# Loads of the next image's first two pairs of chunks, moved ahead by four steps of the image

## The chip, the cores and the metric

The kernel runs on one core of one Trainium2 chip. The metric is the time of one execution on the device in microseconds (us). Before the change it was measured in seven runs; the profile is of one further execution.

The engines are PE (matrix products and transposes), PEld (its weight loads), DVE (elementwise on vectors), ACT (activations), POOL (indirect gathers, powers) and SP (nothing but DMA issues). ACT and POOL issue DMAs as well.

## The reference

The input x is (4, 32, 128, 128) in float32: four images. Layer 0 turns each image into 128 channels of 64 x 64 = 4096 positions, and lets every position attend to every other. Layer 1 is linear attention and a mixture of experts, each on normalised tokens and added to its input. Cut to what matters:

```python
def _L0_conv_ref(x, gamma):                 # per image: q is 128 x 4096
    xs = x.reshape(B, C, h, R, w, R).transpose(0, 1, 3, 5, 2, 4).reshape(B, C * R * R, h, w)
    q = xs.reshape(B, C * R * R, hw)
    energy = jnp.einsum('bci,bcj->bij', q, q)
    d = jnp.sqrt(jnp.diagonal(energy, axis1=1, axis2=2))
    energy = energy / (d[:, :, None] * d[:, None, :])
    attn = jax.nn.softmax(energy, axis=-1)
    out = gamma * jnp.einsum('bcj,bij->bci', q, attn) + xs
...
t = t + linear_attention(_ln_t(t))          # 8 heads, K^T V first, no softmax
t = t + experts(_ln_t(t))                   # softmax router, best 2 of 8, weighted sum
```

## The kernel before

**Layer 0.** The 4096 positions of an image are cut into 8 chunks of 512 (NCH), each of 4 blocks of 128 (NJ). Two neighbouring chunks, a pair kc = 0 to 3, are made ready by `prep(b, kc, st)`:

- its first step issues four DMA loads of 128 KB into the tile xx, on SP's queue (L278, inside `load_tokens`);
- it passes some idle units (L298), and then makes two groups of four transposes on PE (tiles ptq, L312), which DVE copies to qT (L301);
- DVE squares and sums (L323, L324), POOL takes the inverse root (L163), and DVE scales the chunks by it (qs, L337);
- two groups of four PE transposes (ptn, L345) follow, which ACT copies to qn (L343).

The tile xx of images 1 to 3 has one buffer. Both qT and qn must stand before the image's rows use them.

`attend(b, st)` runs over the rows i = 0 to 7 of chunks. As the energies are symmetric, only the chunks jc up to i are computed. A step makes two products of qn with qn (pe, L557), takes exp on ACT (pr, L560), and adds pr times qT to the row's sum (po, L439). The other triangle needs the transposed exps: DVE transposes pr in 32 x 32 blocks into the tile F_i_jc (L368), SP stores F to memory in one DMA of 1 MB (blocks<-F, L482), and three ticks later it loads it back in six DMAs with the blocks exchanged (F<-blocks, L494). A while later (LAG, 57 blocks of the clock) PE multiplies F with qT (pg, L374, and L395 for the diagonal), and DVE adds that to the sum o (L384). There are six buffers of F. F_7_1 is the tile of row 7 and chunk 1, blocks_7_2 the store of F_7_2.

**Layer 1** of image b begins at t = 84 and runs on beside the rows of image b+1, one step every ten blocks of the clock. What meets the change is its DMAs: xn<-xs (L1022, SP) brings sorted rows, ys<-xn and ys<-result (L1044, SP) stores the experts' products, POOL gathers them (L1123), acc<-t (L1099) fetches the residual on ACT's queue, DVE adds (L1092, "combine"), and SP stores the output in four DMAs (out_dram<-acc, L1105). In image 0, `setup_sorting` also fills the buffer xs with rows of x by DMAs on ACT's queue (L153), and `input_rows` loads the tile T (L278 too).

**Order.** The main loop at the end of the kernel issues everything, in the order in which it runs. Its clock counts blocks of the image's products; t is that clock in per cent of the image. Generators such as `prep` are listed in `timed` as (generator, begin, end, count): from t = begin on, it is stepped at a rate of count steps for (end - begin) per cent. A pair of `yield` in `prep` is therefore one unit of time, and `idle(n)` passes n such units. Each engine then works its list off in order, and waits there for what an instruction needs. The DMAs of SP and ACT take turns on eight semaphores, in the order of the program; one is issued only when the one eight places ahead of it has landed.

The two lines that place the next image's first pairs are L1341 and L1342, beside the idle units of L298.

Of the kernel before, what the change touches and what calls it, by code (L numbers as in the profile page):

```python
# [22 lines left out]
def kernel(  # L23
# [111 lines left out]
    def setup_sorting():  # L135
        def iota(dst, pattern, part=0):
            nc.gpsimd.iota(
                dst, pattern=pattern, base=0, channel_multiplier=part, allow_small_or_imprecise_dtypes=True
            )

        iota(rank_below, [[1, P]], part=-1)
        nc.vector.tensor_scalar(rank_below, rank_below, 0.0, None, ALU.is_gt)
        iota(upto, [[1, E], [-1, E]])
        nc.vector.tensor_scalar(upto, upto, 0.0, None, ALU.is_ge)
        iota(tiles_of[:, 0, :], [[P, HR]])
        iota(tile_no[:, :, 0], [[1, NT]])
        yield
        yield

        rows = x.rearrange("b c h w -> (b c h) w")  # L150
        step = NT * P // 8
        for g in range(16):
            inst = nc.scalar.dma_start(xs[g // 8][ts(g % 8, step), :], rows[ts(g, step), :])  # L153
            xs_made[g // 8].append(inst.ins)
            yield
            yield
# [5 lines left out]
    def pow_neg_half(dst, src):  # L162
        pinned(nc.gpsimd.tensor_tensor(dst, src, neg_half.to_broadcast(list(src.shape)), ALU.pow))  # L163
# [13 lines left out]
    def idle(n):  # L177
        for _ in range(2 * n):
            yield

    def keep_running(n, pool=None, tag=None):

        bank = psum_t("spare") if pool is None else pool.tile([P, CH], F32, tag=tag, name="spare")
        for _ in range(n):
            nc.tensor.transpose(bank[:, :P], ident, ident)
# [4 lines left out]
    def hold(name, evict, alloc=psum_t):  # L190


        while len(held) >= banks[0]:
            held[0]()
        bank = alloc(name)

        def done():
            if done in held:
                held.remove(done)
                evict(bank)  # L200

        held.append(done)
        return bank, done
# [69 lines left out]
    def load_tokens(dst, b, k0, nk, queues=(nc.sync, nc.sync)):  # L273
        src = tokens(x, b)
        for r1 in range(2):
            for s in range(2):
                p0 = s * 64 + r1 * 32
                queues[r1].dma_start(dst[p0 : p0 + 32], src[s, r1, :, k0 : k0 + nk, :])  # L278


    def prep(b, kc, st):

        if b == 0:
            if kc == 0:
                st["all"] = big1.tile([P, 4, 8, HW2, 2], F32, tag="T", name="xx_0")
            xx = st["all"][:, kc]
        else:
            xx = xin.tile([P, 8, HW2, 2], F32, tag="xx", name=f"xx_{b}_{kc}")
        first = b == 0 and kc == 0
        load_tokens(  # L290
            xx.rearrange("p k w r -> p k (w r)"), b, 8 * kc, 8, (nc.sync, nc.scalar if first else nc.sync)
        )
        qT = qpool.tile([P, 2, NJ, P], F32, tag="qT", name=f"qT_{b}_{kc}")
        st.setdefault("qT", {})[2 * kc] = qT[:, 0]
        st["qT"][2 * kc + 1] = qT[:, 1]
        yield
        yield
        yield from idle(2 if b else 1)  # L298

        def load_half(g, pt):  # L300
            nc.vector.tensor_copy(  # L301
                qT[:, :, 2 * g : 2 * g + 2, :].rearrange("p s j (r c) -> p (j r) s c", c=64),
                pt.rearrange("p (m s c) -> p m s c", s=2, c=64),
            )

        for g in range(2):
            yield
            pt, done = hold(f"ptq_{b}_{kc}_{g}", partial(load_half, g))
            for jj in range(2):
                for r2 in range(2):  # L310
                    k = 4 * g + 2 * jj
                    nc.tensor.transpose(  # L312
                        pt[:, ts(2 * jj + r2, P)], xx[:, k : k + 2, :, r2].rearrange("p k w -> p (k w)"), ident
                    )
            yield
            done()
        yield
        yield
        ss = stat.tile([P, 2 * NJ], F32, tag="ss", name=f"ss_{b}_{kc}")
        rn = stat.tile([P, 2 * NJ, 1], F32, tag="rn", name=f"rn_{b}_{kc}")  # L320
        for s in range(2):
            sq = work.tile([P, NJ, P], F32, tag="qs", name=f"sq_{b}_{kc}_{s}", bufs=2)
            nc.vector.tensor_tensor(sq, qT[:, s], qT[:, s], ALU.mult)  # L323
            nc.vector.tensor_reduce(ss[:, ts(s, NJ)], sq, AX.X, ALU.add)  # L324
            if first:
                pow_neg_half(rn[:, ts(s, NJ), 0], ss[:, ts(s, NJ)])
            elif s == 1:
                pow_neg_half(rn[:, :, 0], ss)
            yield
            yield  # L330
        yield from idle(1)
        if first:
            keep_running(22, ps_g, "pg")
        scaled = []
        for s in range(2):
            qs = work.tile([P, NJ, P], F32, tag="qs", name=f"qs_{b}_{kc}_{s}", bufs=2)
            nc.vector.tensor_tensor(qs, qT[:, s], rn[:, ts(s, NJ)].to_broadcast([P, NJ, P]), ALU.mult)  # L337
            scaled.append(qs)
        for s, qs in enumerate(scaled):
            yield  # L340
            qn = npool.tile([P, CH], F32, tag="qn", name=f"qn_{b}_{2 * kc + s}")
            st.setdefault("qn", {})[2 * kc + s] = qn
            pt, done = hold(f"ptn_{b}_{kc}_{s}", lambda p, qn=qn: nc.scalar.activation(qn, p, AF.Copy))  # L343
            for j in range(NJ):
                nc.tensor.transpose(pt[:, ts(j, P)], qs[:, j, :], ident)  # L345
            yield
            done()
        yield
        yield
# [233 lines left out]
    def finish():  # L583

        while queued or late:
            yield
            tick[0] += 1
            turn_tick()
            clock[0] += 3 * NJ
            step_share()  # L590
            yield


    def input_rows(b, st):
        st["T"] = T = big1.tile([P, KT, D], F32, tag="T", name=f"T_{b}")
        nk = 4 if b == 0 else 8
        for k in range(0, KT, nk):
            load_tokens(T[:, k : k + nk, :], b, k, nk)
            yield
            yield  # L600
            yield from idle(1)
# [729 lines left out]
    timed = [(first, 0, 1, 4)]  # L1331
    for b in range(B):

        if b == 0:
            for kc, begin, end in ((1, 0, 5), (2, 6, 20), (3, 25, 45)):
                timed.append((prep(0, kc, states[0]), begin, end, 12))
            timed.append((setup_weights(), 46, 58, 9))
            timed.append((setup_sorting(), 58, 98, 17))
        if b + 1 < B:
            nxt = states[b + 1]  # L1340
            timed.append((prep(b + 1, 0, nxt), 65, 82, 13))  # L1341
            timed.append((prep(b + 1, 1, nxt), 87, 99, 13))  # L1342
        begin, end, count = (52, 94, 17) if b == 0 else (36, 47, 9)
        timed.append((input_rows(b, states[b]), begin, end, count))
        done = [0] * len(timed)
        start = clock[0]
        closing = None
        for half, _ in enumerate(chain(attend(b, states[b]), finish() if b == B - 1 else ())):
            if half % 2 == 0:
                t = 100 * (clock[0] - start) / UNITS  # L1350
                moved = []
                if closing is None and t > 84:
                    closing = layer1(b, states[b])
                    steady.append([closing.first_parts() if b == B - 1 else closing.all_parts(), clock[0]])
                for n, (steps, begin, end, count) in enumerate(timed):
                    if t >= begin and done[n] * (end - begin) < (t - begin) * count:
                        moved.append(steps)
                        done[n] += 1
                for stream in steady:
                    if clock[0] >= stream[1]:  # L1360
                        stream[1] = clock[0] + PACE
                        moved.append(stream[0])
            for steps in moved:
                next(steps, None)
        for steps, *_ in timed:
            for _ in steps:
                pass
        timed = []
        if b + 1 < B:
            timed.append((prep(b + 1, 2, nxt), 2, 20, 13))  # L1370
            timed.append((prep(b + 1, 3, nxt), 30, 50, 13))
# [43 lines left out]
```

## Time and profile before

| | us |
|---|---|
| median of 7 runs | 1696.12 |
| lowest and highest of them | 1694.2 and 1701.56 |
| profiled execution | 1698.16 |
| its span, first to last instruction | 1696.4 |
| mean granted PE clock in the span | 0.994 |
| PE waiting at ptq (L312) for xx | 11.1 in 3 places |
| PE waiting at ptn (L345) for qs | 7.0 in 3 places |
| PE waiting at pg (L374) for F<-blocks | 1.2 in 1 place |

The profile gives the busy time of each engine in the span, groups of like instructions by line, and for an engine's idle time what ended it. A line such as "PE ptq L312 <- DMA xx<-in_x_dram" is PE idle ahead of the matmul at L312 that writes ptq, until a load of xx landed. In a timeline, "x4" is four like instructions shown as one, and the bracket at the end is the idle time before it. SPq and ACTq are the queues' issuing instructions; their time is that of the issue, not of the transfer. The granted clock is PE's share of full speed. Of the three waits at ptq and at ptn, one each (5.8 and 0.9 us) lies at the start of the program, where image 0 is loaded.

### The profile page before, as it was taken

The numbers are of one execution on the slowest core, as the hardware profiler recorded it, in microseconds if no ns is written. First come the engines' busy times: TensorE is split into PE (matmuls) and PEld (weight loads), VectorE is DVE, ScalarE is ACT, GpSimd is POOL, SyncE is SP. The second block draws the span as 40 slices with busy tenths as digits, with TensorE's granted clock in tenths as the row PEclk, the third lists the DMA queues.
The fourth block names the chain that finished last, engine by engine and source line by source line (L and its number), as shares of the span: only waits on it lengthen the run. The fifth ranks groups of instructions, "written<-read, shape, count | busy, mean of one in ns | idle before, by whom it ended". The sixth has DMA issues, their size and how long they took to land.

```text
span 1696.4 us, 21941 instructions
## 1 busy us (share of the span) xinstructions
PE 1646.7 (97%) x5458; PEld 878.5 (52%) x5458; DVE 934.8 (55%) x2443; ACT 927.8 (55%) x2893; POOL 511.1 (30%) x553
## 2 busy tenths in 40 slices
PE   8999999999999999989999999999999999999888
PEld 5444444455554555545564455544555455554643
DVE  4434334367485335477478334557748633455686
ACT  3555445565565555546565555545556555555376
POOL 1000000011027425451014641544102742445167
PEclk9999999999999999999999999999999999999999
DMA  4554756754458778875457777886435966885001
GB/s 132 172 171 164 202 174 211 246 198 162 139 168 281 227 234 247 248 216 175 147 177 230 237 233 241 246 262 198 164 137 168 285 223 221 249 249 145 7 10 41
DMA packets 227341, 323.94 MB, mean 191 GB/s; under 512 B 31760, under 2 KB 155792, under 8 KB 213136
## 3 DMA queue, kind: packets, MB, share of 16 engines
q1 hardware_dynamic: 206704, 283.57, 52.9%
q0 software_dynamic: 12288, 25.19, 5.1%
q10 hardware_dynamic: 8224, 13.77, 2.8%
q8 instruction: 46, 0.75, 0.2%
q14 instruction: 79, 0.65, 0.1%
HBM read 152.28 MB, written 173.15 MB: 192 GB/s over the span
## 4 chain that ended last, share of the span: by engine, by line
PE 81%; DVE 8%; DMA 4%; ACT 3%; issue 1%; POOL 1%; SPq 1%; ACTq 0%; DVEq 0%; POOLq 0%
PE po L439 23%; PE pe L557 22%; PE pg L374 19%; PE pys L1058 3%; PE py L1207 2%; PE pg L395 2%; DMA F<-blocks 2%; PE pys L1065 2%; PE pat L803 1%; PE pgram L677 1%; ACT xn L645 1%; DVE df L710 1%; DVE F L368 1%; PE ptq L312 1%; PE ptn L345 1%
## 5 line engine op out<-in xcount | busy, mean ns | idle before, releaser
L560 ACT ACTIVATE pr<-pe 128x512 f32<-128x512 f32 (+1 forms) x576 | 322.4, 560 | 541.0 <-PE pe L557 501.0
L439 PE MATMUL po<-pr,qT 128*128 128x512 f32 (+3 forms) x1152 | 550.9, 560 | 3.9 <-ACT o L444 3.7
L557 PE MATMUL pe<-qn,qn 128*128 128x512 f32 x896 | 461.6, 597 | 1.9 <-ACT pr L560 1.6
L374 PE MATMUL pg<-F,qT 128*128 128x512 f32 x864 | 441.7, 593 | 2.0 <-DMA F<-blocks 1.2
L368 DVE STREAM_TRANSPOSE F<-pr 128x512 f32<-128x512 f32 x440 | 306.1, 702 | 150.6 <-ACT pr L560 141.3
L439 PEld LDWEIGHTS po<-pr,qT 128*128 128x128 f32 x1152 | 216.5, 191 | 250.3 <-issue 220.5
L379 ACT ACTIVATE junk<-F 128x512 bf16<-128x512 f32 x432 | 268.0, 620 | 2.3 <-DMA F<-blocks 1.4
L374 PEld LDWEIGHTS pg<-F,qT 128*128 128x128 f32 x864 | 164.3, 191 | 194.6 <-issue 178.4
L1123 POOL DMA_INDIRECT yb<-ys,place x192 | 185.7, 967 | 241.2 <-ACT pr L560 66.7
L996 POOL DMA_INDIRECT xs<-xn,place x192 | 185.6, 967 | 157.4 <-ACT pr L560 93.8
L557 PEld LDWEIGHTS pe<-qn,qn 128*128 128x128 f32 x896 | 154.9, 192 | 109.0 <-issue 101.4
L384 DVE TENSOR_TENSOR o<-o,pg 128x512 f32<-128x512 f32 x110 | 75.5, 686 | 204.3 <-PE pg L374 204.1
L163 POOL TENSOR_TENSOR rn<-ss,neg_half 128x8 f32<-128x8 f32 (+1 forms) x17 | 26.9, 1585 | 332.6 <-DVE ss L324 332.5
L560 ACT ACTIVATION_READ_ACCUMULATOR pr<-pe 128x1 f32 x576 | 111.9, 194 | 0.0
L1032 ACT ACTIVATE xn<-pys 128x256 f32<-128x256 f32 x120 | 45.2, 377 | 108.6 <-PE pys L1065 108.4
L163 POOL TENSOR_TENSOR rsf<-dm_f,neg_half 128x8 f32<-128x8 f32 (+1 forms) x15 | 26.2, 1746 | 235.1 <-DVE sv_f L637 235.1
L1058 PEld LDWEIGHTS pys<-ew_sb,xn 128*128 128x128 f32 x468 | 69.7, 192 | 46.5 <-issue 43.5
L557 PE MATMUL pe<-qn 128*128 128x512 f32 (+3 forms) x256 | 90.8, 437 | 0.7 <-ACT qn L343 0.7
L163 POOL TENSOR_TENSOR rsa<-dm_a,neg_half 128x8 f32<-128x8 f32 x16 | 26.4, 1648 | 191.0 <-DVE sv_a L637 190.6
L379 ACT ACTIVATION_READ_ACCUMULATOR junk<-F 128x1 f32 x432 | 83.0, 192 | 0.0
L1041 DVE COPY xn<-pys 128x256 f32<-128x256 f32 x60 | 25.4, 424 | 88.0 <-ACT xn L1032 86.4
L1041 DVE COPY result<-pys 128x256 f32<-128x256 f32 (+1 forms) x60 | 24.6, 410 | 88.9 <-ACT xn L1032 79.8
(216 smaller groups left out, 1672.2 us busy)
## 6 DMA issues: line engine op xcount, KB each, us to landing
blocks<-F SPq DMA_DIRECT2D x108, 1024.0 KB
F<-blocks SPq DMA_DIRECT2D x216, 192.0 KB
F<-blocks SPq DMA_DIRECT2D x216, 128.0 KB
xn<-xs SPq DMA_DIRECT2D x114, 128.0 KB
F<-blocks SPq DMA_DIRECT2D x216, 64.0 KB
below<-F SPq DMA_DIRECT2D x31, 384.0 KB
out_dram<-acc SPq DMA_DIRECT2D x128, 64.0 KB
xx<-in_x_dram SPq DMA_DIRECT2D x62, 128.0 KB
```

What stands on the lines that cost most here:

```text
L163: pinned(nc.gpsimd.tensor_tensor(dst, src, neg_half.to_broadcast(list(src.shape)), ALU.pow))
L368: f()
L374: nc.tensor.matmul(pg.rearrange("p (a f) -> p a f", a=4), st["qT"][i][:, ib, :], G[:, :, ib], start=(ib == 0), stop=(ib == NJ - 1),)
L379: nc.scalar.activation(junk, G[:, :, ib], AF.Copy, accum_out=st["sums"][:, NJ * i + ib, jc : jc + 1])
L384: nc.vector.tensor_tensor(o, o, pg.rearrange("p (a j c) -> p a j c", a=4, c=S), ALU.add)
L439: nc.tensor.matmul(row["po"][:, lo:hi], qT[blk // NJ][:, blk % NJ, :], w, start=start, stop=(row["left"] == 0))
L557: nc.tensor.matmul(pe[:, c0:], qn[jc][:, ts(j, P)], qn[i][:, c0:], start=True, stop=True)
L560: nc.scalar.activation(pr[:, c0:], pe[:, c0:], AF.Exp, accum_out=sums[:, t, i : i + 1]).ins
L996: inst = nc.gpsimd.indirect_dma_start(xs[h], offset(place[:, i, k : k + 1]), xn[:, k, :], None)
L1041: nc.vector.tensor_copy(result[:, :n], p[:, 2 * P : 2 * P + n * D].rearrange("p (j c) -> p j c", c=D))
L1058: nc.tensor.matmul(p[:, 2 * P + j * D : 2 * P + j * D + D], bufs[4 + g % 2][:, j, :], weights[:, bass.ds(begins[2 * (g % 2) + j], D)], sta ...
L1123: inst = nc.gpsimd.indirect_dma_start(yb[k // 4][:, i, k % 4, :], None, ys, offset(place[:, i, k : k + 1]))
```

## The change

In images 1 to 3, the pairs kc = 0 and 1 idle for six units instead of two between the loads and the first transposes. Their generators begin earlier by about as much, with 17 steps in the time from the new begin: the loads of kc = 0 go out from t = 60 instead of 65, those of kc = 1 from 83 instead of 87 (t of the image before). The transposes stay at about the same t: for kc = 0 the step number n falls at 65 + 17n/13 before and at 60 + 22(n + 4)/17 after; for kc = 1 at 87 + 12n/13 and 83 + 16(n + 4)/17. In all, 24 loads of 128 KB move: two groups of four while image 0, 1 and 2 is computed. Pairs kc = 2 and 3 and image 0's own pairs are as before.

```diff
@@ -295,7 +295,7 @@
         st["qT"][2 * kc + 1] = qT[:, 1]
         yield
         yield
-        yield from idle(2 if b else 1)
+        yield from idle((6 if kc < 2 else 2) if b else 1)
 
         def load_half(g, pt):
             nc.vector.tensor_copy(
@@ -1338,8 +1338,8 @@
             timed.append((setup_sorting(), 58, 98, 17))
         if b + 1 < B:
             nxt = states[b + 1]
-            timed.append((prep(b + 1, 0, nxt), 65, 82, 13))
-            timed.append((prep(b + 1, 1, nxt), 87, 99, 13))
+            timed.append((prep(b + 1, 0, nxt), 60, 82, 17))
+            timed.append((prep(b + 1, 1, nxt), 83, 99, 17))
         begin, end, count = (52, 94, 17) if b == 0 else (36, 47, 9)
         timed.append((input_rows(b, states[b]), begin, end, count))
         done = [0] * len(timed)
```

## The prediction

> **What bounds the kernel now.** I began with the page's busy times and its chain that ended last.
>
> ```profile
> PE 1646.7 (97%) x5458; PEld 878.5 (52%) x5458; DVE 934.8 (55%) x2443; ACT 927.8 (55%) x2893; POOL 511.1 (30%) x553
> PE 81%; DVE 8%; DMA 4%; ACT 3%; issue 1%; POOL 1%; SPq 1%; ACTq 0%; DVEq 0%; POOLq 0%
> ```
>
> PE is busy for 97% of the span, so only PE's gaps and its clock can move the end. Next I read what PE waits for, and what SP waits for.
>
> ```profile
> PE ptq L312 <- DMA xx<-in_x_dram: 11.1, 3, 5.8
> PE ptn L345 <- DVE qs L337: 7.0, 3, 3.1
> ...
> SPq L278 <- DMA xs<-in_x_dram: 21.9, 4, 6.3
> ...
> SPq L494 <- DMA acc<-t: 18.8, 5, 4.5
> ```
>
> The columns are total us, times, longest. Both PE rows belong to `prep`. The last two rows show that SP's issues wait for transfers issued by ACT with which they share no data. The lists of both kernels say why: the DMAs of SP and ACT, counted together in program order, take turns on eight semaphores, and each first waits for the one eight places ahead.
>
> PE's timeline gives the places (start, duration, idle time before in brackets):
>
> ```profile
> 717.17 1.02 PE L374 MATMUL pg<-F,qT 128*128 128x512 f32 x2
> ...
> 723.42 0.88 PE L312 MATMUL ptq<-ident,xx 128*128 128x128 f32 x4 [2.65 <-DMA xx<-in_x_dram]
> ...
> 747.85 1.12 PE L345 MATMUL ptn<-ident,qs 128*128 128x128 f32 x4 [3.09 <-DVE qs L337]
> ...
> 1127.61 0.72 PE L312 MATMUL ptq<-ident,xx 128*128 128x128 f32 x4 [2.64 <-DMA xx<-in_x_dram]
> ...
> 1150.35 1.03 PE L345 MATMUL ptn<-ident,qs 128*128 128x128 f32 x4 [3.09 <-DVE qs L337]
> ```
>
> Call the gaps at 723.42 and 1127.61 A: the chunk pair kc=1 of the next image isn't there. Call those at 747.85 and 1150.35 B: the scaled chunks come late from DVE. The chain around the first A and B and SP's queue there:
>
> ```profile
> 711.37 3.43 DMA acc<-t
> 715.25 0.43 SPq L278
> ...
> 718.03 5.25 DMA xx<-in_x_dram
> 723.42 0.88 PE ptq L312 x4
> 724.30 1.71 PE pe L557 x2
> 726.00 1.53 PE po L439 x2
> 727.54 0.86 PE pg L374 x2
> ...
> 732.09 0.68 DVE qT L301
> ```
>
> ```profile
> 708.47 2.74 SPq L494 DMA_DIRECT2D F<-blocks  x6
> 714.86 0.34 SPq L482 DMA_DIRECT2D blocks<-F  x1
> 715.25 3.28 SPq L278 DMA_DIRECT2D xx<-in_x_dram  x4
> ...
> 720.62 4.54 SPq L494 DMA_DIRECT2D F<-blocks  x6
> ```
>
> The store blocks<-F at 714.86 stands eight places behind the fetch acc<-t (L1099), which ACT issues at 711.37 and which lands at 714.80. SP stands still for it, and the four xx loads behind come late. In the chain, pe and po take 1.71 and 1.53 after the gap instead of 0.86 a pair. The granted clock says why (third figure from the end):
>
> ```profile
> 723.00:728.00 5.00, 4.58 (x10) 2.42 (x11) 3.13 (x7) 1.30 (x4) 0.96 (x1) 0.66 1.01 288
> 1127.00:1131.00 4.00, 3.39 (x13) 2.00 (x14) 2.56 (x7) 1.30 (x4) 0.82 (x1) 1.00 1.09 272
> ```
>
> After both B it is 0.66 too. So three of the four gaps were followed by a lower clock, and the fourth was not. One drop costs 0.85 (pe) + 0.67 (po) + 0.16 (ptq, 0.88 against 0.72 at full clock) = 1.7 us.
>
> **The change, part by part.** No arithmetic is added. Six groups of four 128 KB loads (24 issues on SP, 0.4 to 0.5 us each in these rows where none waits) go ahead in SP's queue; the instructions behind them keep their t. ACT's and POOL's lists are unchanged in order. PE's differs by one group of ptn moved three places behind, DVE's by the copy and scaling steps of `prep`.
>
> *Removed: A.* The kc=1 loads of images 2 and 3 now stand right behind F_7_0's six loads (700.0 and some 1105.0), 21 us ahead of their transposes. The slowest xx load near here took 6.7 us (715.73 to 722.38), so A goes: 2.65 + 2.64, and one clock drop: 1.7. Sum: -7.0.
>
> *Added: a wait at pg.* Four more DMAs ahead shift every semaphore slot by four until the old place. They pass out stores, ys stores, blocks_7_1 and F_7_1's loads. The slot of acc<-t, which blocks_7_2 had, falls to the first of F_7_1's six loads (L494). These had gone out at 708.47 and landed by 714.14, 3.0 us ahead of the pg at 717.17. Now they wait for acc<-t. ACT still issues this at 711.37, behind its exp; such fetches took 2.9 to 3.5 us, so it lands at 714.3 to 714.9. The nearest groups of six loads took 5.0 (361.42 to 366.43) to 6.2 us (731.34 to 737.54) from first issue to last landing: 719.3 to 721.1. PE waits 2.1 to 3.9 us; I take 3.0. In image 2 the fetch goes out at 1115.57 and pg stands at 1121.37, again 2.1 to 3.9. Behind the waiting loads on SP are blocks_7_2, out stores and F_7_2's loads; those go out no later than before, since SP stood at 714.86 anyway, and F_7_2 has over 2.5 us to spare. So: 2 x 3.0, and by the count of three gaps in four, 2 x 0.75 x 1.7 = 2.6. Sum: +8.6, bounds 4.2 and 11.2.
>
> *Moved on DVE: B.* Ahead of B, DVE works without a gap from 731.48 to 747.85. The list of the change has the copy qT L301 (732.09, 0.68 us) ahead of work that ran at 726, where DVE then idles 3.9 us until 731.48. So the backlog, and B, shrink by 0.65 each: -1.3. The rest, 2.4 us, is shorter than any gap seen to lower the clock or not; I halve its chance, 2 x 0.5 x 1.7 = -1.7. Bounds of the clock: 0 and -3.4. If the cover is gone (the copy itself late), B stays and the sum is 3.0 higher.
>
> *Image 0.* The last kc=0 load of image 1 takes the slot of an xs fetch (L153) that ACT issues at 237.78 and that lands at 240.88; blocks_6_1 behind goes from 232.72 to some 241.3. Of F_6_1's six loads five then wait for the xs fetch issued at 245.91, with 3.1 to 5.7 us to land. I estimate F_6_1 whole at 252.3 to 252.8, against 247.87 before and its pg at 251.70: +1.0, bounds 0 and 1.4, too short for a clock drop. The kc=1 loads there make F_7_2 land near 330 against 331.98: nothing, but each us over 2 would count. The kc=0 loads of images 2 and 3 delay xn loads by 0.8 us against some 7 to spare: nothing.
>
> Sum: -7.0 + 8.6 - 3.0 + 1.0 = -0.4 us. The profiled execution took 1698.16 (span 1696.4 and 1.8 around it), 2.0 above the median, so 1697.8 there and 1695.8 as median.
>
> Two rules of the Trainium skill say otherwise. "TensorE: Matmul & The Clock Gate", part 1 on the HAM clock gate, has the clock halve after at least one idle window of about 3.4 us. No gap here is that long, yet the rows show 0.66 after 2.65; by the page the sum would be -5.3 + 6.0 - 1.3 + 1.0 = +0.4. "DMA: Bandwidth & Descriptors", rules for kernel authors, advises to issue a DMA early and wait late; by that alone the wait at pg isn't there and the sum is -9.0. The SP row at 714.86 speaks against it, since here the early issue hands its slot to someone else.
>
> **Rivals.** *Faster: the wait at pg doesn't bite.* Then -7.0 - 3.0 + 1.0 = -9.0, median 1687.1. For it: five groups of L494 already wait for acc<-t (18.8 us in all), and PE lost only 1.2 us to F<-blocks in the whole span. Against: it needs F_7_1 down by 717.17, 2.4 us after acc<-t landed, while the quickest six took 5.0. It would need another order of slots than the list has.
>
> *Slower: F_7_1's loads run as slowly as F_7_2's did.* Those took 7.4 us (720.62 to 728.06), since they shared the engines with xx, out stores and a blocks store. From 714.86 this gives 722.3: a gap of 5.1 each, surely with the lower clock: 2 x 6.8 - 7.0 - 3.0 + 1.0 = +4.6, median 1700.7. It decides from a landing after 721.7 (gap 4.5, sum +3.4). For it: the DMA share is 0.86 at 715 to 720. Against: the xx loads, which filled that stretch, have gone ahead.
>
> *It doesn't do what it says:* the xx loads are held where they are. For it: SP does stand at slots. Against: their own slots belong to ys stores and F_7_0's loads, down by 701.8. Time as before.
>
> **How the numbers follow.** Some 0.2% (3.4 us) is what a measurement of this kernel can tell from no change. The forecast's own range: low end -7.0 + 4.2 - 4.7 + 0 = -7.5 (1688.6), high end -7.0 + 11.2 - 1.3 + 1.4 = +4.3 (1700.4); the ends need every term at once. Forecast 0.62, of which 0.06 beyond 0.2% on either side; faster rival 0.15, slower rival 0.20, no effect 0.03. So faster 0.21, same 0.53, slower 0.26. The range of 8 in 10 leaves out most of the faster rival and the upper half of the slower one: 1690 to 1701.
>
> **What would show it.** Right: PE's waits lose two of the three ptq rows; a row pg L374 <- DMA F<-blocks of some 2 to 4 us appears twice, at 717 to 721 and at 1121 to 1125; SP shows L494 waiting for acc<-t there; B reads about 2.4. A pg wait near 252 of about 1 us is the price of image 0. Wrong: no pg wait (then faster by 9), a pg wait of 5 (slower), or B unchanged or longer.

## The result, and the profile after

The changed kernel takes 1699.21 us (median of 26 runs), the kernel before 1697.6 (63 runs). The ratio of the two, from all runs and not from the medians alone, is 1.0013, with a 95% interval of 1.0005 to 1.0020; the ratios below are of the same kind. So the change makes the kernel 2.2 us slower, between 0.8 and 3.4, where a sum of -0.4 had been forecast. The profiled execution took 1700.63, its span is 1698.9 against 1696.4.

What PE waits for in the changed kernel (total us, times, longest):

```profile
PE pg L374 <- DMA F<-blocks: 10.0, 4, 3.7
PE ptq L312 <- DMA xx<-in_x_dram: 5.9, 1, 5.9
PE ptn L345 <- DVE qs L337: 5.7, 3, 2.3
```

The two ptq waits A are gone, as the change meant (the 5.9 left is at the start of the program), and the two ptn waits B are 0.75 us shorter each. In their place pg waits for F<-blocks: 10.0 us in place of 1.2. PE's timeline shows where (start, duration, idle time before in brackets):

```profile
253.80 1.10 PE L374 MATMUL pg<-F,qT 128*128 128x512 f32 x2 [1.73 <-DMA F<-blocks]
...
722.54 1.10 PE L374 MATMUL pg<-F,qT 128*128 128x512 f32 x2 [3.38 <-DMA F<-blocks]
...
749.65 0.65 PE L345 MATMUL ptn<-ident,qs 128*128 128x128 f32 x4 [2.34 <-DVE qs L337]
...
1127.32 2.05 PE L374 MATMUL pg<-F,qT 128*128 128x512 f32 x2 [3.69 <-DMA F<-blocks]
...
1155.69 0.66 PE L345 MATMUL ptn<-ident,qs 128*128 128x128 f32 x4 [2.34 <-DVE qs L337]
```

The chain of waits says how the first of the long ones comes about:

```profile
712.29 0.87 PE pe L557 x2
...
713.20 2.65 DMA acc<-t
...
715.91 0.31 SPq L494
```

And SP's queue there:

```profile
700.21 2.81 SPq L494 DMA_DIRECT2D F<-blocks  x6
703.05 2.06 SPq L278 DMA_DIRECT2D xx<-in_x_dram  x4
...
711.95 0.92 SPq L1044 DMA_DIRECT2D ys<-result  x2
715.91 2.66 SPq L494 DMA_DIRECT2D F<-blocks  x6
718.66 0.37 SPq L482 DMA_DIRECT2D blocks<-F  x1
```

SP is done with the ys stores at 712.9 and then stands until 715.91: F_7_1's first load waits for acc<-t, which ACT issued with its exp and which landed at 715.85. The last of the six loads landed at 722.23, and pg started at 722.54. In image 0 SP's queue ahead of the wait at 253.80 is:

```profile
233.00 8.34 SPq L278 DMA_DIRECT2D xx<-in_x_dram  x4
241.44 0.40 SPq L482 DMA_DIRECT2D blocks<-F  x1
241.88 3.49 SPq L278 DMA_DIRECT2D T<-in_x_dram  x4
247.49 3.44 SPq L494 DMA_DIRECT2D F<-blocks  x6
```

The last of the four xx loads stands at the slot of an xs fetch until 241.03, and the store blocks_6_1 goes out only behind it. The clock after the gaps (third figure from the end):

```profile
723.00:728.00 5.00, 5.00 (x11) 2.18 (x10) 0.00 (x0) 1.48 (x6) 3.08 (x4) 0.66 0.85 248
1128.00:1133.00 5.00, 5.00 (x7) 2.02 (x6) 0.00 (x0) 1.30 (x4) 0.93 (x1) 0.50 0.77 232
749.00:754.00 5.00, 4.34 (x10) 2.23 (x11) 4.79 (x18) 1.79 (x5) 3.62 (x3) 0.70 0.70 256
1155.00:1160.00 5.00, 4.31 (x13) 2.21 (x14) 4.57 (x18) 1.78 (x5) 2.51 (x2) 1.00 0.73 261
```

After both long pg waits PE runs at half speed, after the second for twice as long (the clock's records show 6.83 us at 0.5 in place of 3.41); after B once of two. A stretch of 3.41 us at half speed costs some 1.7 us and is called a drop here. Matmul for matmul, PE is 1.7 us behind the kernel before at 496 (image 0), 1.9 at 900 (image 1) and 3.65 at 1303 (image 2); in the last image's tail, which the change doesn't touch, 1.2 us come back.

### The profile page after: what moved, and what is told of

It reads as the page before. It is cut to its first block, busy times and chain, and to the rows that moved or that the text cites. A ratio compares the mean times of both kernels' runs of the same rounds, so it can differ in the third digit from the quotient of the medians.

```text
span 1698.9 us, 21928 instructions
## 1 busy us (share of the span) xinstructions
PE 1648.7 (97%) x5458; PEld 875.7 (52%) x5458; DVE 934.5 (55%) x2443; ACT 928.5 (55%) x2893; POOL 511.6 (30%) x553
## 4 chain that ended last, share of the span: by engine, by line
PE 79%; DVE 7%; DMA 6%; ACT 3%; SPq 2%; issue 1%; POOL 1%; ACTq 0%; DVEq 0%; POOLq 0%
PE po L439 22%; PE pe L557 22%; PE pg L374 19%; PE pys L1058 3%; PE py L1207 2%; DMA F<-blocks 2%; PE pg L395 2%; DMA blocks<-F 2%; PE pys L1065 2%; SPq L494 1%; PE pat L803 1%; ACT xn L645 1%; PE pgram L677 1%; DVE F L368 1%; PE ptq L312 1%
```

## The experiments

The theory: the new wait is F_7_1's first load standing at the semaphore slot of the residual's fetch acc_4, which ACT issues late. The rivals: the xx bytes, now earlier, crowd the transfers of F; the distance alone decides; and, for B and image 0, others named below. All ratios are to the kernel before. In the lists of DMAs (SP and ACT together, in program order) the one that inherits acc_4's slot in images 1 and 2 is:

| kernel | kc=1 ahead by | inherits the slot | new pg waits | ratio (interval) |
|---|---|---|---|---|
| before | 0 | blocks_7_2, xx behind it | none, A 2.65 and 2.64 | 1 |
| kc1_two_steps | 2 | third load of F_7_1 | 1.19 and 1.51 | 0.9977 (0.9968 to 0.9986) |
| kc1_images23 | 4 | first load of F_7_1 | 2.97 and 3.51 | 1.0017 (1.0005 to 1.0028) |
| kc1_five_steps | 5 | an output store | none over 0.5 on a DMA | 0.9945 (0.9930 to 0.9961) |
| kc1_six_steps | 6 | blocks_7_2, xx far ahead | 0.6 at most | 0.9943 (0.9929 to 0.9958) |

**only_kc0: the half for kc=0 alone.**

```diff
-        yield from idle(2 if b else 1)
+        yield from idle((6 if kc == 0 else 2) if b else 1)
-            timed.append((prep(b + 1, 0, nxt), 65, 82, 13))
+            timed.append((prep(b + 1, 0, nxt), 60, 82, 17))
```

> Only the loads of kc=0 move ahead (begin 60, six idle units); those of kc=1 stay as before. Slot theory: in image 0 the same wait of 1.7 us at pg for F_6_1 near 254 as in the changed kernel, since the last kc=0 load holds the slot of an xs fetch that ACT issues late; in images 1 and 2 both A waits at ptq (2.6 each) and both B waits (3.1) are there as before and no pg wait. Time: 1.5 us above the kernel before (0.0 to 0.15 per cent slower). Rival, the xx bytes crowd the transfers of F: pg waits at other places too, in images 1 and 2 near 600 to 620 and 1000 to 1020, and 3 us or more above before.

1.0023 (1.0012 to 1.0033): 3.9 us slower, a miss: 1.5 was expected. A and B are as before, and no wait appears in images 1 and 2. Image 0's wait is 2.3 us here and drew a clock drop:

```profile
253.00:257.00 4.00, 3.24 (x4) 1.40 (x5) 0.00 (x0) 0.72 (x2) 0.00 (x0) 0.61 0.38 153
```

So kc=0's move costs, and only in image 0; the price there is at the edge where the clock begins to fall.

**kc1_images23: kc=1 of images 2 and 3 alone.**

```diff
-        yield from idle(2 if b else 1)
+        yield from idle((6 if kc == 1 and b > 1 else 2) if b else 1)
-            timed.append((prep(b + 1, 1, nxt), 87, 99, 13))
+            timed.append((prep(b + 1, 1, nxt), 83, 99, 17) if b else (prep(b + 1, 1, nxt), 87, 99, 13))
```

> Only the loads of kc=1 of images 2 and 3 move ahead (begin 83, six idle units); kc=0 and image 1's kc=1 stay as before. Slot theory: no pg wait near 254, both pg waits for F_7_1 as in the changed kernel (3.4 and 3.7 us, followed by the lower clock), no A, B 2.3 each. Time: 1.6 us below the changed kernel, so 0 to 1 us above the kernel before. Rival, the pg waits of images 1 and 2 come from image 0's delay: they fall under 2 us and the time is 4 us or more below before.

No wait near 254, both pg waits there (2.97 and 3.51), so these don't come from image 0's delay. The time is a miss: 1.0017, 2.9 us above before where 0 to 1 was expected. In its profiled execution neither pg wait was followed by a lower clock, and that one was the quickest of its eleven (1695.46, the others up to 1704.74); so the clock is the likely difference. Only that one execution has a trace, but the mean granted clock of each is on record: over the eleven it is some 0.001 lower than over the 23 of the kernel before on the same chip (0.9926 and 0.9937). That is worth 1.7 us, uncertain by about as much, so the clock may be most of the 2.9 us; it isn't shown to be.

**fetch4_later: the change, with acc_4's fetch three steps later.** The xx loads stay where the change put them.

```diff
-                    after_steps.append((now[0] + 1, partial(fetch, k // 4)))
+                    after_steps.append((now[0] + (3 if k // 4 == 4 else 1), partial(fetch, k // 4)))
```

> The changed kernel with one thing more: the residual's fetch acc_4 (L1099) of each image is issued three steps of the experts later, so that it stands behind F_7_1's loads and blocks_7_2 in the order of the DMAs. The xx loads stay where the change put them. Slot theory: F_7_1's loads go out at some 713 instead of 716 and both pg waits (3.4, 3.7) fall below 0.5 us with the clock drops behind them; F_7_2's third load now holds that slot, so a new wait of 0 to 2 us at F_7_2's pg may appear. Time: 6 to 11 us below the changed kernel (0.3 to 0.6 per cent faster than before). Rival, the xx bytes that now run at 703 to 708 slow F_7_1: both pg waits stay over 2.5 us and the time stays at the changed kernel's.

0.9942 (0.9929 to 0.9955): 9 to 10 us faster than before, by one line on the change that moves no load. SP's queue in image 1:

```profile
712.12 0.91 SPq L1044 DMA_DIRECT2D ys<-result  x2
713.12 2.75 SPq L494 DMA_DIRECT2D F<-blocks  x6
715.96 0.38 SPq L482 DMA_DIRECT2D blocks<-F  x1
```

F_7_1's loads go out right behind the ys stores; the two long pg waits are gone, with xx at its new place. What is left of pg's waits (3.3 us) is image 0's 2.15 and less than 1 each elsewhere. The time is some 11 to 12 us below the changed kernel's, at the upper end of the 6 to 11 expected or a little over it. The crowding rival falls.

**kc1_six_steps and kc1_five_steps: two and one steps further ahead than four.** kc=1 of images 2 and 3 alone, with eight idle units and (81.36, 99, 19), or seven and (82.3, 99, 18), in place of six and (83, 99, 17).

> The kernel before with kc=1 of images 2 and 3 moved ahead by six steps instead of four (eight idle units, begin 81.4). The same 24 fewer loads as in the run with only these moved, but now acc_4's slot falls to blocks_7_2, as in the kernel before, and not to a load of F_7_1. Slot theory: no A, no pg wait, no clock drop there; blocks_7_2 waits for acc_4 until some 715 and costs nothing; B 2.3 or less. Time: 7 to 11 us below the kernel before. Rival, loads moved further ahead crowd F more: pg waits as in the changed kernel or longer, time at or above before.

> The kernel before with kc=1 of images 2 and 3 moved ahead by five steps (seven idle units, begin 82.3): one step from the changed kernel's four on one side, one from the six on the other. acc_4 now stands behind the first of F_7_1's loads and its slot falls to an output store. Slot theory: no A, no pg wait over 0.5 us, time 7 to 11 us below before, as with six steps. Rival, the distance decides: pg waits between those of four and six steps, 1.5 to 2 us each, time 2 to 5 us below before.

Eight loads move in each of these, not 24. 0.9943 and 0.9945: 9 to 10 us faster. Between four steps and five the time falls by some 12 us at once, and between five and six it stays, so the distance as such doesn't decide. In the first, blocks_7_2 stood until 715.75, as in the kernel before, and no pg wait over 0.6 followed; B was 1.5 and 2.5, the second a little over the 2.3 expected:

```profile
709.49 2.73 SPq L494 DMA_DIRECT2D F<-blocks  x6
715.75 0.34 SPq L482 DMA_DIRECT2D blocks<-F  x1
```

**kc1_two_steps.** Four idle units and (85.12, 99, 15).

> The kernel before with kc=1 of images 2 and 3 moved ahead by two steps (four idle units, begin 85.12). acc_4's slot falls to the third of F_7_1's six loads. Slot theory: no A, but pg waits of 2.0 to 3.5 us for F_7_1 in images 1 and 2, about as in the changed kernel; image 0 as before. Time: 4 us below to 1 above before. Rival, what counts is only how early the loads go: no pg wait, the time 6 to 9 us below before.

0.9977, 3.9 us faster. A is gone and the pg waits are there, but shorter than the 2.0 to 3.5 expected: 1.19 and 1.51. A likely reason, not tested alone, is that two loads go out ahead of the one that waits, and only four remain behind acc_4. B stays at 3.0 and 3.1.

**fetch4_later_alone: the same one line on the kernel before, no load moved.**

> The kernel before with no load moved; only the residual's fetch acc_4 is issued three steps of the experts later, so that it stands behind blocks_7_2. Slot theory: A came from blocks_7_2 standing at acc_4's slot with the xx loads behind it; now blocks_7_2 and xx go out at 711 to 713, the xx loads land by 719, 4 us ahead of their transposes, and both A (2.6 each) go with no load moved; a new wait of up to 1 us at F_7_2 or F_7_3 may appear. B 2.3 to 3.1. Time: 5 to 9 us below before. Rival, A came from the load's place in the program: both A stay over 2 us and the time is that of before.

0.9942 (0.9929 to 0.9956): 9.9 us faster, where 5 to 9 were expected. blocks_7_2 goes out 4.6 us sooner, the xx loads behind it too, and A is gone:

```profile
706.47 3.72 SPq L494 DMA_DIRECT2D F<-blocks  x6
710.29 0.37 SPq L482 DMA_DIRECT2D blocks<-F  x1
710.70 3.57 SPq L278 DMA_DIRECT2D xx<-in_x_dram  x4
```

So A, which the change set out to remove, goes without moving a load. It came from the late fetch together with the loads' place behind the store that held its slot, and changing either removes it.

**six_steps_early_scaling: kc1_six_steps with six idle units instead of eight,** so that kc=1's transposes and scaling come two steps earlier.

> As kc1_six_steps, but with six idle units instead of eight, so that the transposes, squares and the scaling of kc=1 in images 2 and 3 come two steps earlier in DVE's list, ahead of the block of L710, L732 and L735 behind which the scaling (L337) stood. Theory of B: B (1.5 and 2.5 us in kc1_six_steps) is the wait for that DVE backlog; it falls below 0.5 us each. Time: 2 to 5 us below kc1_six_steps, 10 to 14 below before. Rival, B is the wait for POOL's inverse root or for DVE's load as such: B stays over 1.5 us and the time is that of kc1_six_steps.

0.9903 (0.9888 to 0.9918), 1680.59 us: 16 us faster than before, more than the 10 to 14 expected, and the fastest version here. In kc1_six_steps POOL's root and DVE's work in image 1 were:

```profile
733.36 1.67 POOL L163 TENSOR_TENSOR rn<-ss,neg_half 128x8 f32<-128x8 f32 x1 [1.24 <-DVE ss L324]
...
733.77 2.78 DVE L710 TENSOR_TENSOR df<-o,pbd 64x512 f32<-64x512 f32 x4
...
741.21 1.29 DVE L337 TENSOR_TENSOR qs<-qT,rn 128x512 f32<-128x512 f32 x2
```

The root was there at 735.03, 6 us ahead of the scaling, so the wait wasn't for POOL. Now DVE has:

```profile
731.54 1.24 DVE L337 TENSOR_TENSOR qs<-qT,rn 128x512 f32<-128x512 f32 x2
...
733.36 2.81 DVE L710 TENSOR_TENSOR df<-o,pbd 64x512 f32<-64x512 f32 x4
```

The scaling now stands ahead of L710, L732 and L735, and the wait at ptn falls from 1.5 and 2.5 us to 0.3 in the whole span (the start's included). So B was that backlog.

**images23_only: the change without image 1's pairs.** Both kc of images 2 and 3 as in the change, those of image 1 as before.

> The change with image 1's two pairs left as before: only the loads of kc=0 and kc=1 of images 2 and 3 move. Theory: image 0's pg wait near 254 (1.7 us in the changed kernel) is gone, kc=0's move in images 1 and 2 costs PE nothing (no wait of 0.5 us or more near 600 to 625 and 1005 to 1030 that the kernel before hasn't), both pg waits for F_7_1 stay (3.0 to 3.7 us), B 2.3 each. Waits: 6.5 to 7.1 new against 5.3 of A and 1.5 of B gone, clock drops about as often as before, so 0 to 2 us above the kernel before. Rival, the long pg waits cost more clock than A did, as the median of kc1_images23 had it: 2 to 4 us above.

0.9993 (0.9979 to 1.0006), on a chip on which the kernel before took 1709.75. Image 0's wait is gone, the pg waits stay (3.15 and 3.26); B is 3.6 in image 1, where 2.3 was expected, and 2.3 in image 2. The interval (3.6 us below to 1.0 above) holds the lower half of the 0 to 2 us expected and leaves out the rival's 2 to 4. So without image 0's part the change can't be told from the kernel before.

The single runs don't add up, though. kc1_images23 has nearly the same long waits and came out 2.9 us above; with the 3.9 of only_kc0 that makes 6.8, beside 2.2 for the whole change. By its waits alone kc1_images23 should be 0.3 us below the kernel before. Part of this may be the clock (1.7 us by its records, above) and chance; the rest stays open.

**kc0_three_steps: kc=0 of image 1 alone, three steps instead of four.** One execution on the same chip.

> The kernel before with kc=0 of image 1 alone moved ahead by three steps (five idle units, begin 61.07) instead of the change's four; images 2 and 3 as before. The last xx load still stands at the slot of the late xs fetch, but blocks_6_1 now stands ahead of the four loads. Slot theory of image 0's wait (blocks_6_1 goes out 8 us late behind the held load): blocks_6_1 goes out near 232 as before, and the pg wait for F_6_1 near 253 (1.7 in the changed kernel, 2.3 in only_kc0) falls to 0 to 0.8 us. Rival, the xx bytes and T loads crowd the transfers, or F_6_1's own slot holds it: the wait stays over 1.4 us.

The wait is 1.01 us: between the two answers, which were 0 to 0.8 and over 1.4. SP's queue:

```profile
232.50 0.42 SPq L482 DMA_DIRECT2D blocks<-F  x1
232.96 8.43 SPq L278 DMA_DIRECT2D xx<-in_x_dram  x4
241.44 3.04 SPq L278 DMA_DIRECT2D T<-in_x_dram  x4
244.59 6.03 SPq L494 DMA_DIRECT2D F<-blocks  x6
```

blocks_6_1 goes out at 232.50, in the changed kernel at 241.44; so some of the 1.7 to 2.3 us was that store. But the fifth load of F_6_1 then waits for the next xs fetch (issued 245.55, landed 249.83; the load goes out at 249.85). Both slots belong to image 0's price; how much each holds of it alone wasn't separated further.

## Why the prediction was wrong

In images 1 and 2 the mechanism was right: the slot, the places and the waits. The sizes of three terms were wrong (the pg waits, the clock, image 0), and in image 0 the wait was put down to the wrong DMA. The sum against one pair of profiles, with one clock drop at 1.7 us:

| step | put down | measured |
|---|---|---|
| A gone, with its one clock drop | -7.0 | -5.3 - 1.7 = -7.0 |
| pg waits for F_7_1 | +6.0 | 3.38 + 3.69 = +7.1 |
| clock after them | +2.6 | 3 drops' time: +5.1 |
| B shorter | -1.3 | 4.68 - 6.18 = -1.5 |
| clock after B | -1.7 | one drop of two left: -1.7 |
| image 0 | +1.0 | +1.7 |
| sum | -0.4 | +3.7 |

PE was 3.65 us behind at 1303, so the measured column closes for this pair. How many drops an execution gets is partly chance (see the last section): by the estimate there the change gains and loses about none on average. Then the clock's -0.8 in the forecast (-1.7 of A, +2.6, -1.7 of B) should have been about 0, and the waits' +0.4 (-5.3 + 6.0 - 1.3 + 1.0) was +2.0 (pg 1.1 more, image 0 0.7 more, B 0.2 less). Together that takes -0.4 to about +2.

**Right:** A's removal; that the residual's fetch acc_4 makes the wait, and that its slot falls to F_7_1's first load; both places; B's 0.65 each (0.75) by the copy that leaves the backlog; that kc=0 in images 1 and 2 and kc=1 in image 0 cost nothing. **The faster rival** needed another order of slots, and kc1_five_steps and kc1_six_steps are such orders: they gave the 9 us that it was put down with. **The slower rival** had F_7_1 landing at 722.3; it landed at 722.23, but by luck: the loads went out at 715.91, not at 714.86, and took 6.3 us, not 7.4. pg's own place had moved from 717.17 to some 719.2 with image 0's delay, so the gap wasn't 5.1.

**Where it failed:**

- *"The nearest groups of six loads took 5.0 (361.42 to 366.43) to 6.2 us"*, and from this *"PE waits 2.1 to 3.9 us; I take 3.0."* They took 6.3 us (715.91 to 722.23) and 6.4 (1120.60 to 1127.02), a little over the upper row. The waits were 3.38 and 3.69, inside the bounds but at the upper end both times. The fetch itself was taken too narrowly: *"such fetches took 2.9 to 3.5 us"* leaves out fetches of 4.2 to 6.2 us in the same profile, but here they took 2.65 and 2.87, so this cost nothing.
- *"by the count of three gaps in four, 2 x 0.75 x 1.7 = 2.6."* The count was of four gaps of another length, and one drop was taken to be all that a gap can cost. The gap of 3.69 us cost two in this profile.
- *"I estimate F_6_1 whole at 252.3 to 252.8"*, and *"+1.0, bounds 0 and 1.4, too short for a clock drop."* It was whole at 253.44. blocks_6_1, issued at 241.44 with four T loads behind it, took 5.9 us to land (247.35), where 4.4 had been the row before; F_6_1's loads went out only then, at 247.49. So the loads waited for their own data. The xs fetch that the prediction had five of them wait for was issued at 246.11 and had landed at 249.26, before the load at its slot had its turn (250.04). The wait was 1.7 here and 2.3 in only_kc0, with a drop.
- The place of the slot was explained too simply: it isn't that everything shifts by four. In the combined list F_7_1's first load went from place 665 to 669, and acc_4 from 663 to 661, so the load went from two places behind the fetch to eight. By the shift of four alone the slot would have fallen to the third load.
- *"those go out no later than before"*, said of the DMAs behind the waiting loads, was wrong as well: F_7_2's loads went out at 724.83 where it had been 720.62. PE found F_7_2 there even so, so nothing was lost.

All three sizes erred the same way, and the forecast of no change stood on a sum of -0.4 whose largest terms were -7.0 and +8.6.

## What to carry to other kernels

Where DMA issues of several queues share a ring of semaphores, ask of each stalled load first whose landing it waits for: moving the load hands the slot on to another DMA, and moving the late holder of the slot (one line here) can remove the wait. A wait that is only moved isn't paid for by its length alone; look at where the clock falls. And when two large terms nearly cancel, the answer lies in the sizes: bound each by the row with the same traffic around it, not by the middle of the near ones.

## What the runs showed of the hardware

*The clock falls on idle time within a window, not on the length of a gap.* In all profiles the granted clock changes on a grid of 3.41 us, whose start against the program differs from run to run. Over the 84 gaps of PE of over 1.2 us behind the first 100 us in the twelve profiles, cut by that grid: where one window held 2.05 us or more of a gap, the next ran at half speed, 44 times of 44; with 1.82 or less, once of 32; between, two of 8. So in the kernel before the gap A of 2.65 us drew a drop and that of 2.64 didn't: the second was split into 1.63 and 1.02. The Trainium skill ("TensorE: Matmul & The Clock Gate", part 1 on the HAM clock gate) gives the same free-running window of 3413 ns, but asks for at least one idle window; here some 2 us in one suffice. Taken as a rule (2.0 us within one window of 3.41, the grid falling anywhere with equal chance), a gap g from 2.0 to 3.4 us draws a drop with an estimated chance of (g - 0.6) / 3.4: 0.60 for A, 0.73 for B before, 0.82 for 3.38, 0.51 for B after, and by the same counting 0.91 for 3.69. That is 2.7 drops before and 2.75 after, so by this estimate the clock gave the change nothing on average. The records of whole executions agree: the mean granted clock is 0.9932 over 28 of the changed kernel, and 0.9937 (23) and 0.9930 (15) over those of the kernel before on two chips. The waits alone (7.1 + 1.7 - 5.3 - 1.5) make +2.0 us, beside the measured 2.2. The estimate doesn't account for kc1_images23, where it too has no more drops than before.

*A gap that spills into the next window can cost two.* Three times the clock stayed at half for 6.83 us, two drops in a row: the window that followed the long idle one still held 0.73, 0.89 and 1.11 us of the gap. With 0.65 us or less there, the clock came back after one.
